# Layer 0 of a four-layer graph kernel: the second diffusion product of a period moved half a period on, block ends moved later in the order, and the guess and the column lists cut into pieces

## The chip, the cores and the metric

The kernel runs on one core of a Trainium2 chip. The time is the device time of the whole program in microseconds; before the change the median of three runs is 3632.99 us (3631.25 to 3634.81).

## The reference

There are N = 4096 nodes with 256 features, and a sparse 4096 x 4096 matrix `adj` (about five entries in a row). Four layers follow each other, each on `h = relu(layernorm(x))` and each added to `x`. The change concerns layer 0 alone, which is cut here to what it computes:

```python
R = S + eye; R = R / R.sum(-1)                 # S is adj
Z = 0; Xf = X; Xa = X
for n in range(2):
    probs = softmax((Xa @ W1.T @ W2.T) @ (Xa @ W3.T).T)
    A = probs * (smallest set of entries of the row that holds 0.9 of its sum)
    A = A / A.sum(-1)
    Xf = R @ Xf                                # diffusion, sparse
    Xa = A @ Xa                                # attention, dense
    Z = Z + Xf @ U1[n].T + Xa @ U2[n].T
out = layernorm(X + Z)
```

The search for the set is what is dear: for each of the 4096 rows of `probs` a threshold has to be found above which 0.9 of the sum lies. Layers 1 to 3 are a graph convolution, a graph attention with four heads and another convolution.

## The kernel before, in words

Layer 0 has two steps, n = 0 and n = 1, each a call of `layer0_step`. A step goes over 32 blocks of 128 rows, and a software pipeline handles five blocks at once. `period(b)` is one turn of it: block b-1 ends, block b is searched exactly and cut, block b+1 gets the upper bound of its threshold, block b+2 is searched by steps, and block b+3 enters. Step 0 has periods -3 to 31, step 1 periods -3 to 33.

The instructions of VectorE (DVE), ScalarE (ACT) and TensorE (PE) stand on each engine in the order in which `period` calls them: these three are under a manual schedule. The orders of GpSimd (POOL) and of SyncE (SP), which issues most DMAs, are made by the scheduler of the language. [...]

What a period does, by engine, with the lines of the kernel before:

- The first search. `exponentials` (L1117, ACT) makes e = exp(logits - guess) of a block, 128 x 4096. `evaluate(b, k)` (L1133, ACT) runs one pass with Sign and one with Relu over e, on 1024 columns for k = 0 and 1 and on all 4096 for k = 2 and 3; each adds up along the row. `update(b, k)` (L1163 to L1203, then `stepped`, L1178 to L1184, DVE) makes the next threshold of both sums; `measured` reads the sum of Sign in L1163 and that of Relu in L1165. `bound` (DVE) makes the upper bound of the threshold.
- The exact search. `below` (L1286, DVE) clears all entries above the bound and writes the 128 x 4096 buffer `near`; `segments` (L1294) takes the eight largest of each of 16 pieces, `listing` (L1305, L1308) sorts the first 48, `decide` finds the last entry kept, `cut` (L1348) and `drop` (L1355) clear the rest of e.
- Attention. `flip(b, g)` (L1395, PE) transposes four 128 x 128 pieces of e, `take` (L1402, ACT) copies them from PSUM, `attend(b, g)` (L1411, PE) multiplies them with the features, for g = 0 to 7. Copies 0 to 3 of a block are made in its own period, copies 4 to 7 in the next one. The copies have three buffers. In step 0 `attended` (L1420, ACT) then scales the product, and `turn`, `next_keys`, `weighted`, `store_xa` and `store_h` make and store what step 1 needs. In step 1 `add_heads` (L1536, DVE) adds the product to a stored sum.
- Diffusion, in step 1 alone. `pair(b)` gives the two blocks that period b diffuses: periods 0 to 15 do the first diffusion (k = 0), periods 17 to 32 the second (k = 1). `reach` gathers the sparse matrix block and the rows that it touches, by indirect DMAs on POOL (L834); it is called two blocks ahead in `mix`, which holds the product (L849, PE). `mixed` (L1513 to L1527, DVE) adds the product to a stored part. For k = 1 `spread` (L1544, ACT) and `finish` (L1553 on DVE, the rest on POOL) normalise the result and store it.

In `period`, both products of a pair are made in the same period: the first after `logits`, the second after `cut`. `spread` and `finish` of the pair before stand ahead of `segments`. Copies 6 and 7 and the products with them stand ahead of the Sign of k = 2:

```python
take(b - 1, (6, 7)); attend(b - 1, 6); attend(b - 1, 7)
for d, k in pair(b - 1):
    if k: spread(d); finish(d)
beside(islice(best, 8), hi)                    # half of the segments
beside(update(b + 2, 1) if new else nothing, hi)
beside(best, hi)
if new: evaluate(b + 2, 2, (AF.Sign,))
if opened: attended(b - 1)                     # step 0
if new: evaluate(b + 2, 2, (AF.Relu,))
```

(Lines are run together here.) `beside(line, *others)` runs one item of each other line after every item of the first; `some(line, k)` runs k items.

Two pieces of work lie around the steps. `guess` makes the first threshold of each block from the second moments of the keys and from all queries: 512 queries at a time are multiplied (L978, PE), combined (L980, DVE) and summed (L985, PE). Its first 512 columns are done at once, and its remaining seven groups in one block after period -3. `listed_columns` lists the non-zero columns of each matrix block from `marks`, which step 0 has collected, in twenty rounds of a maximum and a replacement (L793, L794, DVE). Ten rounds run in `close` at the end of step 0, four after period -3 of step 1, and the rest, with the small operations that make the indices of the gathers, after period -2. `guess` reads all queries from a 128 x 4096 buffer of the pool `e`.

Of the kernel before, what the change touches and what calls it, by code (L numbers as in the profile page):

```python
# [76 lines left out]
P = 128  # L77
N = 4096
# [576 lines left out]
def fast_layers(  # L655
# [304 lines left out]
    def guess(n, pm, qt):  # L960
# [10 lines left out]
        squares, room = {}, e_pool.tile([P, N], F32, name="e")  # L971
        for lo, hi in ((0, 1), (1, 8)):
            for g in range(lo, hi + 1):
                if g < hi:

                    cols = slice(g * 512, (g + 1) * 512)
                    py = ps.tile([P, 512], F32, name="py", tag="pmisc")
                    nc.tensor.matmul(py, mk, qt[:, cols], start=True, stop=True)  # L978
                    squares[g] = room[:, cols]
                    nc.vector.scalar_tensor_tensor(  # L980
                        squares[g], py, mean, qt[:, cols], op0=ALU.add, op1=ALU.mult
                    )
                if g > lo:
                    for r in range(4):
# [6 lines left out]
                        )  # L991
            bs = slice(4 * lo, 4 * hi)
# [20 lines left out]
    def front(h0, kt, xs):  # L1013
# [12 lines left out]
        qt = e_pool.tile([P, N], F32, name="e")  # L1026
        pm = ps1.tile([P, 512], F32, name="pm", tag="pr")
        spread_, scale, shift = (xs.tile([P, NB, k], F32, name=f"x_{k}{i}") for i, k in enumerate((2, 1, 1)))
        turned, pls = {}, {}
# [12 lines left out]
        for i in range(NB + LAG + 4):  # L1042
# [20 lines left out]
            if 0 <= o - 1 < NB:  # L1063
# [5 lines left out]
                nc.vector.tensor_copy(qt[:, b * P : (b + 1) * P], pkq[:, 1, :])  # L1069
                if b % 4 == 3:  # L1070
                    cols = slice((b - 3) * P, (b + 1) * P)
                    nc.sync.dma_start(q_d[0][:, cols], qt[:, cols])
# [8 lines left out]
    def layer0_step(n, va, kt, own, extra=None):  # L1081
# [390 lines left out]
        def next_keys(b, qt=None):  # L1472
# [6 lines left out]
            q = qt[:, cols] if qt is not None else own.tile([P, P], F32, name="q", bufs=2)  # L1479
# [88 lines left out]
        def period(b):  # L1568
# [6 lines left out]
            if n == 1 and b in (0, NB // 2):  # L1575
                reach(0, b // (NB // 2))
                reach(1, b // (NB // 2))
# [6 lines left out]
            if old:  # L1584
# [8 lines left out]
                attend(b - 1, 5)  # L1593
                take(b - 1, (6, 7))
                attend(b - 1, 6)
                attend(b - 1, 7)
            for d, k in pair(b - 1):
                if k:
                    spread(d)
                    finish(d)  # L1600
            beside(islice(best, 8), hi)
            beside(update(b + 2, 1) if new else nothing, hi)
            beside(best, hi)
            if new:
                evaluate(b + 2, 2, (AF.Sign,))
# [17 lines left out]
            )  # L1623
            if next_:
                exponentials(b + 3)
# [14 lines left out]
            for d, k in diffused[1:]:  # L1640
                mix(d, k)
# [22 lines left out]
            extras = [kept(b)] if cur else []  # L1664
            extras += [mixed(d, k) for d, k in diffused[1:]]
# [498 lines left out]
```

## Time and profile before

| | |
|---|---|
| median of three runs | 3632.99 us |
| the profiled execution | 3867.4 us, span 3865.1 us |
| PE, DVE, ACT, POOL busy | 2724.2, 2705.8, 2242.7, 1269.0 us |
| mean granted clock of TensorE | 0.845 |
| first `below` of step 0, first and last of step 1 | 173.8, 1504.3 and 2833.5 us |
| last `below` of step 0 | 1344.7 us |

The times are those of one profiled execution, which is slower than the runs without the profiler. Busy time counts instructions alone; the ends of PE's instructions are modelled. "Idle before" is the time in which an engine had nothing running ahead of an instruction, and the name after the arrow is what released it. A `below` opens each period on DVE, so the periods can be told apart in the trace by line 1286.

### The profile page before, as it was taken

The numbers are of one execution on the slowest core, as the hardware profiler recorded it, in microseconds if no ns is written. First come the engines' busy times: TensorE is split into PE (matmuls) and PEld (weight loads), VectorE is DVE, ScalarE is ACT, GpSimd is POOL, SyncE is SP. The second block draws the span as 40 slices with busy tenths as digits, with TensorE's granted clock in tenths as the row PEclk, the third lists the DMA queues.
The fourth block names the chain that finished last, engine by engine and source line by source line (L and its number), as shares of the span: only waits on it lengthen the run. The fifth ranks groups of instructions, "written<-read, shape, count | busy, mean of one in ns | idle before, by whom it ended". The sixth has DMA issues, their size and how long they took to land. (4 is left out here: it accounts for less than half of the span.)

```text
span 3865.1 us, 43776 instructions
## 1 busy us (share of the span) xinstructions
PE 2724.2 (70%) x12404; PEld 2039.6 (53%) x12404; DVE 2705.8 (70%) x9371; ACT 2242.7 (58%) x3339; POOL 1269.0 (33%) x1342
## 2 busy tenths in 40 slices
PE   6468787877878781677777877767775466688545
PEld 5246565555656550455555655555553354677434
DVE  3399999999999965777778887788754234688200
ACT  3588878888887525666667777677612012577200
POOL 1000000000000003466656435444452663655465
PEclk9688998989899885888889988888887788798777
DMA  3012222121222321233333322222224453444364
GB/s 105 2 56 82 68 76 83 62 86 62 82 70 74 101 76 50 79 90 102 94 89 102 89 60 86 75 86 80 82 69 148 139 167 111 119 125 112 117 186 150
DMA packets 214103, 357.00 MB, mean 92 GB/s; under 512 B 34135, under 2 KB 147292, under 8 KB 213852
## 3 DMA queue, kind: packets, MB, share of 16 engines
q1 hardware_dynamic: 169356, 237.74, 19.3%
q0 software_dynamic: 43520, 116.14, 11.4%
q8 instruction: 101, 1.65, 0.2%
q14 instruction: 150, 1.23, 0.1%
q10 hardware_dynamic: 976, 0.23, 0.0%
HBM read 290.85 MB, written 63.13 MB: 92 GB/s over the span
## 5 line engine op out<-in xcount | busy, mean ns | idle before, releaser
L1133 ACT ACTIVATE unread<-e,next_pair 128x4096 uint8<-128x4096 f32 (+1 forms) x384 | 1097.9, 2859 | 208.6 <-DVE next_pair L1184 103.4
L1402 ACT COPY at<-pat 128x512 f32<-128x512 f32 x512 | 287.3, 584 | 498.9 <-PE pat L1395 205.9
L1411 PE MATMUL pa<-va,at 128*128 128x256 f32 x2048 | 481.4, 391 | 54.4 <-ACT at L1402 49.7
L1411 PE MATMUL pa<-h,at 128*128 128x256 f32 x2048 | 512.5, 411 | 0.0
L1103 PE MATMUL pl<-kt,qb 64*128 64x512 f32 x1024 | 310.6, 716 | 262.8 <-ACT e L1117 174.2
L1411 PEld LDWEIGHTS pa<-h,at 128*128 128x128 f32 x2048 | 423.3, 211 | 63.7
L1411 PEld LDWEIGHTS pa<-va,at 128*128 128x128 f32 x2048 | 392.6, 196 | 112.5 <-ACT at L1402 54.9
L1395 PE MATMUL pat<-ident,e 128*128 128x128 f32 x2048 | 309.2, 298 | 158.7 <-DVE e L1355 90.0
L1296 POOL COPY eighth<-best 128x16 f32<-128x16 f32 x64 | 13.2, 206 | 1215.3 <-DVE best L1294 1181.3
L1294 DVE MAX8 best<-near 128x8 f32<-128x256 f32 x1024 | 407.6, 418 | 4.8
L1395 PEld LDWEIGHTS pat<-ident,e 128*128 128x128 f32 x2048 | 253.9, 153 | 237.2 <-DVE e L1355 120.4
L834 POOL DMA_INDIRECT vg<-v_d,column x320 | 307.2, 960 | 165.2 <-issue 106.0
L849 PE MATMUL acc<-vg,ac 128*128 128x256 f32 x768 | 222.9, 452 | 167.5 <-DVE y L2097 82.3
L849 PE MATMUL pr<-vg,ac 128*128 128x257 f32 (+1 forms) x768 | 244.3, 482 | 133.3 <-DVE h L1522 72.2
L1117 ACT ACTIVATE e<-pl,minus_guess 128x1024 f32<-128x1024 f32 x256 | 282.9, 1111 | 55.6 <-PE pl L1103 28.6
L1103 PEld LDWEIGHTS pl<-kt,qb 64*128 64x128 f32 x1024 | 98.5, 214 | 400.4 <-ACT e L1117 224.4
L849 PEld LDWEIGHTS pr<-vg,ac 128*128 128x128 f32 x768 | 181.3, 243 | 221.6 <-DVE h L1522 91.3
L1286 DVE SCALAR_TENSOR_TENSOR near<-e,end_hi 128x4096 f32<-128x4096 f32 x64 | 286.5, 4477 | 0.1
L1348 DVE SCALAR_TENSOR_TENSOR e<-e,end_t 128x4096 f32<-128x4096 f32 x64 | 286.6, 4478 | 0.0
L849 PEld LDWEIGHTS acc<-vg,ac 128*128 128x128 f32 x768 | 172.8, 232 | 214.5 <-DVE y L2097 85.7
L1355 DVE MATCH_REPLACE8 e<-drop,e 128x4096 f32<-128x4096 f32 x64 | 282.2, 4409 | 0.0
L834 POOL DMA_INDIRECT vg<-mixed_d,column x160 | 210.7, 1317 | 204.8 <-PE pr L853 140.7
(533 smaller groups left out, 4761.7 us busy)
## 6 DMA issues: line engine op xcount, KB each, us to landing
adj<-in_adjt SPq DMA_DIRECT2D x128, 512.0 KB
ac<-adjc_d SPq DMA_DIRECT2D x96, 384.0 KB
adjc_d<-ac SPq DMA_DIRECT2D x32, 384.0 KB
v_d<-v SPq DMA_DIRECT2D x64, 128.0 KB
vg<-v_d SPq DMA_DIRECT2D x64, 128.0 KB
targets<-steep_d SPq DMA_DIRECT2D x32, 256.0 KB
vg<-v_d,column POOLq DMA_INDIRECT x320
table_d<-tab SPq DMA_DIRECT2D x32, 132.0 KB
```

Source lines behind the costliest of these rows:

```text
L834: nc.gpsimd.indirect_dma_start(out, None, rows, bass.IndirectOffsetOnAxis(ap=index, axis=0))
L849: nc.tensor.matmul(acc, ac[:, k, :], v[:, k, :], start=(k == 0), stop=(k == CHUNKS and not own))
L1103: nc.tensor.matmul(pl[:, r, :], s["qb"][rows], kt[rows, j * 512 : (j + 1) * 512], start=True, stop=True,)
L1117: nc.scalar.activation(s["e"][:, j * 1024 : (j + 1) * 1024], pl.rearrange("p r c -> p (r c)"), AF.Exp, bias=minus_guess[:, b : b + 1], acc ...
L1133: nc.scalar.activation(unread[:, :width], s["e"][:, :width], func, bias=s["at"], scale=-1.0, accum_out=s["signs"] if func == AF.Sign else ...
L1286: nc.vector.scalar_tensor_tensor(near, s["e"], end["hi"][:, b : b + 1], s["e"], op0=ALU.is_lt, op1=ALU.mult, accum_out=s["low"])
L1294: nc.vector.max(best[:, k, :], near[:, k * (N // SEG) : (k + 1) * (N // SEG)])
L1348: nc.vector.scalar_tensor_tensor(s["e"], s["e"], last, s["e"], op0=ALU.is_ge, op1=ALU.mult, accum_out=s["held"])
L1355: nc.vector.match_replace(s["e"][:, ::-1], s["drop"], s["e"][:, ::-1], 0.0)
L1395: nc.tensor.transpose(pt[:, k, :], s["e"][:, c * P : (c + 1) * P], ident)
L1402: nc.scalar.copy(at, s["pt", g])
L1411: nc.tensor.matmul(s["pa"], s["at", g][:, k, :], va[:, c, :D], start=(c == 0), stop=(c == NB - 1))
```

## The change

In `period`:

- Copies 6 and 7 of block b-1 and the products with them are called after the Sign of k = 2. `attended` still stands between Sign and Relu in step 0, and now behind them.
- The second product of a pair, `mix`, is called at the end of the period, behind copies 2 and 3; its `mixed` is run in the next period, beside the second half of the segments.
- `spread` and `finish` are called behind `decide`, and ahead of the exponentials.
- The first two `reach` of each diffusion are called after the segments of periods 0 and 16, not at the head of these periods.
- A line `fill` is run in three places of a period, three items in each.

`guess` yields after each group of 512 columns, reads its queries from a buffer of 128 x 512 that it loads from `q_d` (two buffers, the products overwrite them), and keeps the first group in `near`. The lines `guess` and `listed_columns` are run as `fill` in the first periods. `front` and `close` no longer hold a 128 x 4096 buffer of queries. In `front` each group of four blocks is copied to a small buffer that is stored.

```diff
@@ guess
-        squares, room = {}, e_pool.tile([P, N], F32, name="e")
         for lo, hi in ((0, 1), (1, 8)):
+            squares = {}
             for g in range(lo, hi + 1):
                 if g < hi:
-                    cols = slice(g * 512, (g + 1) * 512)
+                    if g == 0:
+                        queries, squares[g] = qt, near[:, 3584:]
+                    else:
+                        queries = squares[g] = wk.tile([P, 512], F32, name="queries")
+                        nc.sync.dma_start(queries, q_d[n][:, g * 512 : (g + 1) * 512])
                     py = ps.tile([P, 512], F32, name="py", tag="pmisc")
-                    nc.tensor.matmul(py, mk, qt[:, cols], start=True, stop=True)
-                    squares[g] = room[:, cols]
+                    nc.tensor.matmul(py, mk, queries, start=True, stop=True)
...
+                    if lo:
+                        yield
@@ period
-        def period(b):
+        def period(b, fill=()):
...
-            if n == 1 and b in (0, NB // 2):
-                reach(0, b // (NB // 2))
-                reach(1, b // (NB // 2))
...
                 attend(b - 1, 4)
                 attend(b - 1, 5)
+            beside(islice(best, 8), hi)
+            beside(update(b + 2, 1) if new else nothing, hi)
+            late = chain(*[mixed(d, k) for d, k in pair(b - 1)[1:]])
+            beside(best, hi, late)
+            some(late, 9)
+            if n == 1 and b in (0, NB // 2):
+                reach(0, b // (NB // 2))
+                reach(1, b // (NB // 2))
+            some(fill, 3)
+            if new:
+                evaluate(b + 2, 2, (AF.Sign,))
+            if old:
                 take(b - 1, (6, 7))
                 attend(b - 1, 6)
                 attend(b - 1, 7)
-            for d, k in pair(b - 1):
-                if k:
-                    spread(d)
-                    finish(d)
-            beside(islice(best, 8), hi)
-            beside(update(b + 2, 1) if new else nothing, hi)
-            beside(best, hi)
-            if new:
-                evaluate(b + 2, 2, (AF.Sign,))
             if opened:
                 attended(b - 1)
...
                 add_heads(b - 1) if old and n == 1 else nothing,
             )
+            for d, k in pair(b - 1):
+                if k:
+                    spread(d)
+                    finish(d)
+            some(fill, 3)
...
                 some(mixed(d, k), 9)
-            for d, k in diffused[1:]:
-                mix(d, k)
...
-            extras = [kept(b)] if cur else []
-            extras += [mixed(d, k) for d, k in diffused[1:]]
-            along(chain(aim(b + 3), update(b + 3, 0)) if next_ else nothing, chain(*extras))
+            for d, k in diffused[1:]:
+                mix(d, k)
+            along(chain(aim(b + 3), update(b + 3, 0)) if next_ else nothing, kept(b) if cur else nothing)
+            some(fill, 3)
@@ the calls
-            period(-3)
-            some(guesses, 2)
-            for b in range(-2, NB):
-                period(b)
+            for b in range(-3, NB):
+                period(b, guesses)
...
+            fill = chain(guesses, lists)
             for b in range(-3, NB + 2):
-                period(b)
-                if b == -3:
-                    some(guesses, 2)
-                    some(lists, 4)
+                period(b, fill)
                 if b == -2:
-                    some(lists, 99)
+                    some(fill, 99)
```

## The prediction

> **What bounds the kernel now.** I read the busy slices first, then busy times by stretch, then the timelines of ScalarE (ACT) and VectorE (DVE) inside one period of each kind. A period opens with the 4.48 us row of line 1286 (`below`). Slices:
>
> ```profile
> PE   6468787877878781677777877767775466688545
> ...
> DVE  3399999999999965777778887788754234688200
> ACT  3588878888887525666667777677612012577200
> ```
>
> Slices are 96.6 us. DVE is full in slices 3 to 13 (step 0 of layer 0), and no engine is in slices 16 to 29 (step 1). Busy time by stretch (PE, PEld, DVE, ACT, POOL, then clock): 23 periods of step 0; step 1's first diffusion; its second diffusion; period 15, which gathers nothing; period 17, where no finished pair is normalised:
>
> ```profile
> 411.10:1274.70 863.60, 694.45 (x3037) 496.85 (x3036) 808.37 (x2877) 701.73 (x875) 10.54 (x69) 0.91 0.23 74
> 1616.40:2241.50 625.10, 478.71 (x2070) 355.79 (x2071) 482.07 (x1812) 427.49 (x481) 363.55 (x306) 0.89 0.33 92
> 2321.20:2750.50 429.30, 317.55 (x1399) 234.94 (x1398) 338.10 (x1251) 296.60 (x361) 201.00 (x221) 0.84 0.28 81
> ...
> 2166.40:2200.90 34.50, 30.43 (x145) 23.60 (x146) 31.56 (x123) 29.34 (x34) 7.27 (x6) 0.95 0.33 102
> 2241.50:2278.10 36.60, 33.22 (x146) 25.95 (x146) 31.61 (x125) 29.31 (x34) 10.58 (x9) 0.85 0.17 47
> ```
>
> So a period takes 863.6/23 = 37.55 us in step 0, 625.1/15 = 41.7 in the first diffusion, 429.3/10 = 42.9 in the second. Step 0, ACT and then DVE (start, duration, group, idle before):
>
> ```profile
> 794.34 0.58 ACT L1402 COPY at<-pat 128x512 f32<-128x512 f32 x1 [1.58 <-PE pat L1395]
> 796.56 0.58 ACT L1402 COPY at<-pat 128x512 f32<-128x512 f32 x1 [1.64 <-PE pa L1411]
> 797.04 3.71 ACT L1133 ACTIVATE unread<-e,next_pair 128x4096 uint8<-128x4096 f32 x1
> ...
> 801.69 0.47 ACT L1420 ACTIVATE xa<-pa,ra 128x256 f32<-128x256 f32 x1 [0.84 <-PE pa L1411]
> 802.06 3.70 ACT L1133 ACTIVATE unread<-e,next_pair 128x4096 uint8<-128x4096 f32 x1
> ...
> 805.88 0.16 DVE L1165 SCALAR_TENSOR_TENSOR next_pair<-twice,gap 128x1 f32<-128x1 f32 x1 [1.70 <-ACT unread L1133]
> ```
>
> The last two copies of a block, Sign, `attended`, Relu stand in that order, and DVE already waits 1.70 us for the Relu. Second diffusion, DVE then ACT:
>
> ```profile
> 2535.84 4.48 DVE L1286 SCALAR_TENSOR_TENSOR near<-e,end_hi 128x4096 f32<-128x4096 f32 x1
> ...
> 2547.88 0.15 DVE L1553 TENSOR_SCALAR var<-var 128x1 f32<-128x1 f32 x1 [7.55 <-ACT junk_sq L1544]
> ...
> 2547.25 0.51 ACT L1544 ACTIVATE junk_sq<-h,minus_mean 128x256 bf16<-128x256 f32 x1
> ...
> 2556.26 3.71 ACT L1133 ACTIVATE unread<-e,next_pair 128x4096 uint8<-128x4096 f32 x1 [7.72 <-DVE next_pair L1184]
> ```
>
> Here `finish` blocks DVE until ACT has copied 6 and 7 and squared; the searches of the next block stand behind it.
>
> [...] here it is 0.50 from 818.5 to 825.3 in step 0, after a window with PE busy 1.09 of 3.4 us, so little work suffices. [...] one during `below` at 1871.8 took 4.22 us against 0.95.
>
> **The change, part by part.**
>
> *A, step 0: copies 6, 7 and the last two products behind the Sign.* Sign needs the DVE update that ended at 796.60 and started at 797.04 behind copy 7: 0.44 us gained, so it ends at 800.4. Copy 6 then ends at 801.0. Products 6 and 7 on PE: 32 matmuls took 7.07, four blocks of columns, so two take 3.54, to 804.6 with the hand-over. `attended`, which stays before the Relu, 0.47 less overlap: 805.0. Relu 3.79: 808.8, plus hand-overs 809.0, against 805.85. That is +3.0 to +3.2 with nothing to hide it: DVE's L1165 stands in order, and `decide`, `cut` (4.48) and `drop` (4.41) queue behind it. The period of 37.55 is 11 clock windows of 3.413 us; 12 would be 40.96, +3.4. I take +3.2. Periods with both the Relu and an old block are 1 to 29: 29 × 3.2 = +93 (lower end 29 × 2.9 = +84; the upper is a rival).
>
> *B, first diffusion, periods 1 to 15.* Removed: the wait of Sign for copy 7 (period 8: update ready at 10.7 us from its start, Sign at 20.4). Added: the second product, 12 matmuls of 2.88 and two of 0.6, less overlap 3.3 us, moves from beside `cut` and `drop` into PE's run from `drop` to product 7. That run, by rows: transposes 8 × 0.52 = 4.1, attention products 8 × 1.77 = 14.2, now 3.3 more, some 21.6 with waits 23. Before, the run to copy 7 (14.7 in period 15) plus 0.5, Sign and Relu (7.5) made 22.7. So the two cancel; PE now also idles some 5 us before `drop` ends, and a cold start costs up to 3.4 (half of the 6.8 us at 0.50). The mixed result (0.65 us of DVE) only moves. The gathers' delays (period 15 without them 34.5, others about 42) are as many as before, elsewhere. I take +0.5 each: +8; bounds -3.5 and +3, so -52 to +45.
>
> *C, second diffusion, periods 18 to 30.* `spread` and `finish` go behind `decide`: the 7.55 + 0.54 us of DVE wait go. ACT has 1.2 us more after the Relu, covered by DVE's 2.2 us of `decide`. Period 17 shows a period without them: 36.6. To it add half of the cold start, 1.7, and 0.7 (an estimate) for GpSimd's eight normalising operations (0.55 to 0.73 each) between DVE's: 39.0. From 42.7 that is -3.7 × 13 = -48, ends -6 (-78) and -2 (-26). Periods 31 to 33: -5. SP's stores of x1 wait for GpSimd later; behind them on SP stand loads of the next period, with some 30 us of room.
>
> *D, between the steps.* Guess pieces took 3.41 us each (paced by PE) and still do; each now also needs a load through SP, two buffers deep, and SP holds the query load of block 0 behind three of them. Ten list rounds of 2.57 now lie under Sign and Relu (7.6) and the exponentials: -15 at the start of period -1. But `reach` now stands behind the segment search of period 0, so 40 gathers at 1.25 us start about 13 us later and delay DVE's dependent operations (1.24 us each from 1538 to 1550) in `listing` and `decide`: +10. I take -5 (-20 to +8). *E, the front and step 0's guess:* the pieces take the time they took; one 512-wide copy more: 0 (-5 to +3).
>
> Sum: +93 + 8 - 48 - 5 - 5 + 0 = **+43**. The profiled execution has a span of 3865.1 us and took 3867.4, 234 above the median of 3633.0; nothing in the page says where the 234 lie, and step 0 and part C show no gather delays, so I carry the difference over unscaled: **3676 us**.
>
> **Rivals.** *R1, faster.* PE's run isn't the limit in the first diffusion: Sign and Relu no longer wait for copy 7 and go on while the gathers delay PE. Place: L1133 behind L1402. For: Sign stood 10 us idle in period 8. Against: product 7 must still end before `add_heads` (L1536), which already waits for PE in nine periods. It decides from 43/15 = 2.9 us below my B, a gain of 2.4 per period; at -3.5 and part C at -6: 93 - 52 - 78 - 10 = -47, 3586. *R2, colder PE in step 0.* Products 4 and 5 end 3 us before copy 6; if that lets the clock fall, products 6 and 7 take up to 3.4 more: 13 windows, 44.4 a period, +6.8 × 29 = +198, in all +148, 3781. For: the fall at 818.5. Against: 3 us is less than a window, busy on both sides. *R3, no change:* B at -2.4 cancels the rest: 3633.
>
> **How the numbers follow.** Mine 0.55 (3635 to 3720), R1 0.22, R2 0.15, R3 0.08. The bound of same, 0.2%, is 7 us, about what a measurement of this kernel can tell. Mine and R2 give slower 0.70; R3 and edges same 0.07; R1 faster 0.23. The range 3590 to 3760 leaves out less than half of R1 and about half of R2, under 2 in 10.
>
> **What would show it.** A right: step 0's period 40.5 to 41, L1165 waiting about 4.8 us, `xa` (L1429 then) waiting over 3 us for PE. B right: about 42 still, PE's wait and not copy 7 ahead of `add_heads`. C right: no wait at `var`, 38 to 40. D right: list rounds between L1165's waits, gathers starting after the first segments. Wrong if `attended` doesn't wait in step 0, if first-diffusion periods fall below 39, or if PE's clock halves twice in a step 0 period.

## The result and the profile after

The changed kernel takes 3825.74 us (median of 4, 3824.95 to 3827.86) against 3632.97 us before: a ratio of 1.0531, 95% interval 1.0513 to 1.0550. It is 193 us slower. The prediction had the sign and not the size: 3676 us, with a range up to 3760.

One thing has to be known before two profiles are laid side by side. The same kernel before took 3632 to 3634 us on three occasions and 3833 to 3863 us on four others. The difference lies in the stages with gathers, step 1 and layers 1 to 3, and not in step 0: where it is there, the text below speaks of a chip with the delay. (No chip stands twice on record, so that it is the chip and not the occasion is likely, and not shown.) The profile of before that the prediction was made from shows the delay; the times of before and all of the changed kernel's above don't. So periods are compared below within one kind of chip alone, and ratios within one group of runs.

The busy slices of the changed kernel (tenths of a slice of 95.6 us, each row one engine; the last row is TensorE's granted clock in tenths):

```profile
PE   6457777777777777736888888888875656688766
...
DVE  3387778888777888858888888888984434588500
ACT  3476667766677765248777777778751311577400
...
PEclk8678888888888888857888888889887889889888
```

DVE had nines through step 0 before. Now no engine has: step 0 waits. The busy time by stretch (length, PE, PEld, which is PE's loading of weights, DVE, ACT, POOL with counts, clock, DMA share, GB/s): 23 periods of step 0, 15 of the first diffusion (periods 2 to 16), 10 of the second:

```profile
451.40:1472.00 1020.60, 772.12 (x3038) 532.00 (x3037) 810.18 (x2877) 703.88 (x875) 10.53 (x69) 0.85 0.20 63
1797.60:2359.30 561.70, 465.10 (x2087) 368.03 (x2088) 474.38 (x1814) 426.95 (x484) 358.60 (x309) 0.86 0.36 104
2430.10:2801.40 371.30, 308.47 (x1401) 244.78 (x1400) 328.31 (x1252) 294.80 (x361) 241.19 (x221) 0.87 0.32 94
```

A step 0 period takes 44.37 us for 37.55, with DVE's work unchanged (810 us for 808 before), and the clock is 0.85 for 0.91. The diffusion periods are 37.4 and 37.1 us. The timeline of ACT, PE and DVE in one step 0 period (start, duration, engine, line, group, idle before and what ended it; the lines are nine higher than before):

```profile
905.26 3.71 ACT L1142 ACTIVATE unread<-e,next_pair 128x4096 uint8<-128x4096 f32 x1 [4.96 <-DVE next_pair L1193]
908.97 1.05 ACT L1411 COPY at<-pat 128x512 f32<-128x512 f32 x2
909.59 6.41 PE L1420 MATMUL pa<-h,at 128*128 128x256 f32 x16 [3.85 <-ACT at L1411]
916.03 0.47 ACT L1429 ACTIVATE xa<-pa,ra 128x256 f32<-128x256 f32 x1 [6.01 <-PE pa L1420]
916.40 3.70 ACT L1142 ACTIVATE unread<-e,next_pair 128x4096 uint8<-128x4096 f32 x1
920.22 0.16 DVE L1174 SCALAR_TENSOR_TENSOR next_pair<-twice,gap 128x1 f32<-128x1 f32 x1 [7.48 <-ACT unread L1142]
```

Before, products 4 to 7 followed each other on PE without a pause, so that two took half of this:

```profile
794.58 7.07 PE L1411 MATMUL pa<-h,at 128*128 128x256 f32 x32
```

Now products 6 and 7 take 6.41 us where the prediction had 3.54, `xa` waits 6.01 us for them between Sign and Relu, and DVE waits 7.48 us for that Relu (1.70 before). In the traces of before and of the changed kernel every stretch of one clock but the last (263 of 264, 347 of 348) lasts a multiple of 3.413 us, so the clock can be read window by window. Four windows of the same period (PE's busy time follows the length; the clock is the last column but two):

```profile
891.20:894.61 3.41, 3.41 (x13) 2.94 (x12) 3.20 (x15) 3.41 (x2) 0.00 (x0) 0.50 0.75 249
904.85:908.26 3.41, 0.88 (x5) 0.43 (x3) 3.41 (x20) 3.00 (x1) 0.00 (x0) 1.00 0.01 2
908.26:911.67 3.41, 2.08 (x5) 1.73 (x6) 3.21 (x19) 1.76 (x4) 0.20 (x1) 0.50 0.00 0
911.67:915.09 3.42, 3.42 (x9) 2.70 (x9) 1.04 (x7) 0.00 (x0) 0.25 (x2) 0.50 0.00 0
```

While copies 6 and 7 stand behind the Sign, PE stands still for 3.85 us, and the clock is at half for the two windows in which it works again. In all, some four of the period's 13 windows are at half clock, where before it was some two of 11 (`b_finish_2` below; the first of the four windows shown is one that has its like there). In the second diffusion DVE's wait for `var` (7.55 us before) is gone, and another stands in its period, for the products that now come late:

```profile
2601.25 0.48 DVE L1545 SCALAR_TENSOR_TENSOR t<-pa,ra,base 128x256 f32<-128x256 f32 x1 [3.98 <-PE pa L1420]
...
2604.50 0.21 DVE L1562 TENSOR_SCALAR var<-var 128x1 f32<-128x1 f32 x2
```

Where the 193 us lie, by the starts of `below` in the profiles (all from chips without the delay; `b_finish_2`, an experiment below, is the kernel before up to its second diffusion, and gives the numbers of before):

| stretch | before | after | difference |
|---|---|---|---|
| to the first `below` | 173.4 | 180.0 | +6.6 |
| step 0, 31 periods | 1169.8 | 1367.1 | +197.3 |
| between the steps, period 0 of step 1 | 206.5 | 215.0 | +8.5 |
| first diffusion, 15 periods | 506.2 | 560.1 | +53.9 |
| second diffusion and the rest | 1571.7 | 1500.9 | -71 |

The last number of before is `b_finish_2`'s 1448.1 us plus the 123.6 us that it is faster than before. The differences sum to 195.

### The profile page after: what moved, and what is told of

It is laid out like the page before. It is cut to its first block, busy times and chain, and to the rows that moved or that the text cites. A ratio compares the mean times of both kernels' runs of the same rounds, so it can differ in the third digit from the quotient of the medians.

```text
span 3823.1 us, 43861 instructions
## 1 busy us (share of the span) xinstructions
PE 2788.5 (73%) x12404; PEld 2085.5 (55%) x12404; DVE 2689.8 (70%) x9372; ACT 2241.6 (59%) x3339; POOL 1308.4 (34%) x1342
## 3 DMA queue, kind: packets, MB, share of 16 engines
q0 software_dynamic: 43520, 116.14, 11.5%
## 5 line engine op out<-in xcount | busy, mean ns | idle before, releaser
L1420 PE MATMUL pa<-h,at 128*128 128x256 f32 x2048 | 575.4, 445 | 113.0 <-ACT at L1411 113.0
L1404 PE MATMUL pat<-ident,e 128*128 128x128 f32 x2048 | 350.9, 328 | 333.1 <-DVE e L1364 269.6
L1420 PEld LDWEIGHTS pa<-h,at 128*128 128x128 f32 x2048 | 460.3, 231 | 202.6 <-ACT at L1411 124.6
L1404 PEld LDWEIGHTS pat<-ident,e 128*128 128x128 f32 x2048 | 291.4, 168 | 420.9 <-DVE e L1364 294.8
L1420 PE MATMUL pa<-va,at 128*128 128x256 f32 x2048 | 500.2, 404 | 0.0
L1420 PEld LDWEIGHTS pa<-va,at 128*128 128x128 f32 x2048 | 414.5, 207 | 60.7 <-ACT at L1411 0.3
L1112 PE MATMUL pl<-kt,qb 64*128 64x512 f32 x1024 | 321.8, 757 | 126.6 <-ACT e L1126 126.6
L834 POOL DMA_INDIRECT vg<-v_d,column x320 | 307.2, 960 | 119.7 <-issue 99.1
L849 PE MATMUL acc<-vg,ac 128*128 128x256 f32 x768 | 233.8, 453 | 88.4 <-DMA vg<-v_d,column 77.6
L834 POOL DMA_INDIRECT vg<-far_d,column x160 | 210.8, 1318 | 181.2 <-DVE near L820 134.5
L2003 PE MATMUL acc<-u,tabg 128*65 128x128 f32 x1536 | 208.3, 291 | 64.2 <-DVE u L1988 62.2
L834 POOL DMA_INDIRECT vg<-mixed_d,column x160 | 204.6, 1279 | 113.6 <-issue 39.3
```

The costliest lines, as they stand in the source:

```text
L834: nc.gpsimd.indirect_dma_start(out, None, rows, bass.IndirectOffsetOnAxis(ap=index, axis=0))
L849: nc.tensor.matmul(acc, ac[:, k, :], v[:, k, :], start=(k == 0), stop=(k == CHUNKS and not own))
L1112: nc.tensor.matmul(pl[:, r, :], s["qb"][rows], kt[rows, j * 512 : (j + 1) * 512], start=True, stop=True,)
L1404: nc.tensor.transpose(pt[:, k, :], s["e"][:, c * P : (c + 1) * P], ident)
L1420: nc.tensor.matmul(s["pa"], s["at", g][:, k, :], va[:, c, :D], start=(c == 0), stop=(c == NB - 1))
```

## Step 0: does the late copy cost it, and is it the clock?

My theory: copies 6 and 7 behind the Sign cost all of step 0's 6.8 us a period, half of it by the clock. The rival: the loss is the clock's alone, or that of `attended` ahead of the Relu.

**b_again** is the kernel before, unchanged.

> The kernel before once more, for a second profile of it: the first one took 234 us longer than its runs. Theory P (in step 0 the late copies and the half clock cost 6.8 us a period, and the first profile of before was delayed in the gathers of step 1 and of layers 1 to 3): a span near 3633, step 0 at 37.55 us a period as in the first profile, the first diffusion near 34.5 instead of 41.7, the second still 42 to 43. Rival Q (the two profiles differ throughout, so that the stages of before and after can't be compared): step 0 other than 37.5.

It took 3830.25 us under the profiler, and the 23 runs of before in its group had a median of 3833.34. So it wasn't the profiler that made the first profile of before longer than the runs. The theory missed, in this.

**a_early** (lines run together):

```diff
+                if n == 0:
+                    take(b - 1, (6, 7)); attend(b - 1, 6); attend(b - 1, 7)
             beside(islice(best, 8), hi)
...
-            if old:
+            if old and n == 1:
                 take(b - 1, (6, 7))
```

> The kernel after, but in step 0 alone copies 6 and 7 and products 6 and 7 stand ahead of the segments again, as before. Theory P: the period of step 0 falls from 44.4 to 37.55, 29 times 6.83 = 198 us less, 3628. Rival Q (other parts of the change, the query buffers or the guess, slow step 0 as well): less than half of that, above 3725.

The period of step 0 is 37.54 us (before 37.55), and the whole 3827.93 us, 0.9984 of before (0.9973 to 0.9994) on a chip with the delay. So this one move is the whole loss of step 0.

**a_warm** puts six products that nothing reads between products 5 and 6.

```diff
+            if opened:
+                warm = ps1.tile([P, 2, D], F32, name="warm", tag="pr")
+                for k in range(6):
+                    nc.tensor.matmul(warm[:, k % 2, :], ident, va[:, k, :], start=True, stop=True)
```

> The kernel after, with six more products of 128x256 on TensorE in step 0 between product 5 and product 6 of each block, into a PSUM buffer that nothing reads: they only keep TensorE busy while copy 6 waits for the Sign. Theory P (3.4 of the 6.8 us are the half clock that the idle time brings): products 6 and 7 take 3.6 instead of 6.4 us, the period is 41.0 and the time 3826 - 29 x 3.4 = 3727. Rival S (the clock is not the cause, the copies' place alone costs 6.8): 44.4 a period and 3826 or more.

The period is 41.4 us (40.6 to 43.1) for 44.4; the ratio is 1.0288 (1.0256 to 1.0320). The timeline of PE and ACT:

```profile
947.97 2.75 PE L1615 MATMUL warm<-h,ident 128*128 128x256 f32 x12
952.25 3.72 PE L1420 MATMUL pa<-h,at 128*128 128x256 f32 x16 [1.52 <-ACT at L1411]
...
956.01 0.47 ACT L1429 ACTIVATE xa<-pa,ra 128x256 f32<-128x256 f32 x1 [3.32 <-PE pa L1420]
```

With the idle stretch down to 1.52 us the clock stays up there (1.00 from 936.4 to 960.3), the two products take 3.72 us, `xa` waits 3.32 us, and the period is 0.4 us over the 40.5 to 41 us that the prediction gave for full clock. So 3 of the 6.8 us are the clock's, and the rival that it is the clock alone falls.

**a_xa_late** leaves the copies late and puts `attended` behind the Relu in step 0.

> The kernel after, but in step 0 the scaling of the attention product stands behind the Relu, so that Relu no longer waits for products 6 and 7; the copies stay late. Theory P (it is this wait in ACT's queue): Relu ends about 19 us into the period, VectorE waits under 2 us for it, the period is 37.5 to 38.5 and the time 3630 to 3660. Rival R (the late products themselves bound the period, through the transposes and stores behind them): 41 or more a period, over 3720.

The period is 41.0 us, not 37.5 (ratio 1.0215, 1.0181 to 1.0249): this gains 3.4 us of the 6.8, in part by the clock, since the two products take 5.41 us there. DVE's wait for the Relu falls to 0.99 us, and the next in the row takes its place (timeline of ACT and DVE):

```profile
955.00 0.37 ACT L1476 COPY hu<-pu 128x256 f32<-128x256 f32 x1 [0.64 <-PE pu L1456]
...
955.40 0.42 DVE L1477 TENSOR_TENSOR hu<-h,pu 128x256 f32<-128x256 f32 x1 [3.43 <-ACT hu L1476]
```

`turn`, the transposes and `weighted` all follow `xa`, and `hu` stands on DVE between `cut` and `drop`. The end of the block is late for whatever comes next, so that the place of `attended` alone isn't the cause either.

## The diffusions: what the moved product costs and the late finish gains

The second group, on a chip with the delay (before: 3850.85 us):

**a_again**, the changed kernel.

> The kernel after once more, beside the others on one chip. Theory P (step 0 loses 6.8 us in each of 29 periods, whatever the chip; the gathers of step 1 and of the later layers are delayed on some chips and not on others): step 0 at 44.4 us a period, 190 to 200 us over before, a ratio near 1.05. Rival H (the loss was one of the chips compared): a ratio within 1 per cent.

It takes 4040.24 us, ratio 1.0481 (1.0451 to 1.0512): 189 us slower there too, so the rival, a loss that only the chips compared had made, falls. Its periods are 44.4, 43.6 and 37.5 us: the first diffusion is slowed by that chip as before's is, the second is not.

**b_finish**, the kernel before with part C alone:

```diff
-            for d, k in pair(b - 1):
-                if k:
-                    spread(d)
-                    finish(d)
             beside(islice(best, 8), hi)
...
                 add_heads(b - 1) if old and n == 1 else nothing,
             )
+            for d, k in pair(b - 1):
+                if k:
+                    spread(d)
+                    finish(d)
```

> The kernel before with one edit: spread and finish behind decide. Theory P (the wait of VectorE for the squares is what the second diffusion loses): its periods fall from 42.5 to 37 or 38, 13 x 5 = 65 us less than before, nothing else moves. Rival I (the gain of after there comes from the moved product or the late copies): still 41 to 43, within 10 us of before.

It takes 3755.70 us, ratio 0.9745 (0.9720 to 0.9771): 95 us faster, twice what part C was given. The second diffusion goes from 43 to 36.1 us a period.

**b_mix_k0**, the kernel before with the second product of the first diffusion alone at the period's end.

> The kernel before with one edit: in the first diffusion the second product of a pair is made at the end of its period, and its mixing runs beside the next segments (the first two gathers of the second diffusion stand behind the segments of period 16, since they read its last rows). Theory P (the product stands in TensorE's run from drop to the last attention product): the first diffusion's periods get 2 to 3.5 us longer, 30 to 50 us over before. Rival J (it is the late copies that lengthen them in after without its late copies in step 0): within 10 us of before.

It takes 3916.15 us, ratio 1.0148 (1.0114 to 1.0181): 65 us slower; 45.8 us a period in the first diffusion where before has 41 (`b_finish`, the same there, has 40.8).

**a_mixback**, the changed kernel with both taken back: copies of step 0 early, products where they were.

> The kernel after with copies 6 and 7 of step 0 early again, and with the second product of both diffusions back beside the first and its mixing back at the end of the period; finish stays late, the copies of step 1 stay late, the guess and the lists stay in pieces. Theory P: the first diffusion's periods are as in before, the second's at 37 to 38, step 0 at 37.5, some 55 us less than before. Rival K (the second diffusion needs the moved product for its gain): its periods 40 or more, and no more than 20 us less than before.

It takes 3774.80 us, ratio 0.9797 (0.9771 to 0.9823): what is left of the change is faster than before, but 19 us slower than `b_finish`. 15 of these are there when the first block of step 1 is cut: the first `below` is at 182.6 us for 175.7, and the stretch between the steps 168.3 us for 158.6 (step 0 is 1.5 us shorter). Its first diffusion, with copies 6 and 7 late and the product where it was, takes 41.8 us a period: on this chip the late copies alone gain nothing there (`b_finish` 40.8), while with the moved product they give back some 2 us (43.6 in `a_again` for 45.8 in `b_mix_k0`).

The third group met a chip without the delay (before: 3632.30 us). **b_finish_2** is `b_finish` again.

> The kernel before with only spread and finish behind decide, once more, to stand beside the others on the same chip and to see it on another chip. Where the gathers delay the operations that wait for them it is 0.972 to 0.977 of before, with 41 us a period in the first diffusion and 35.5 in the second. Where they don't (before near 3633) theory P expects 34 to 35 us a period in the first diffusion, and a smaller gain, 30 to 60 us, since part of before's 42.7 us a period in the second diffusion was the gathers' and not the wait of finish; the rival expects the same 95 us there.

It takes 3508.69 us, ratio 0.9666 (0.9650 to 0.9683). Its two diffusions:

```profile
1583.30:2056.00 472.70, 415.67 (x1962) 320.31 (x1961) 441.33 (x1696) 397.49 (x449) 343.11 (x291) 0.95 0.42 118
2157.70:2495.70 338.00, 299.41 (x1400) 227.26 (x1399) 327.46 (x1251) 294.69 (x361) 245.34 (x220) 0.95 0.36 103
```

These are 14 periods of 33.76 us and 10 of 33.80, now alike. The changed kernel's 37.4 us in the first, which would have passed for a gain against the 41.7 us that the prediction worked with, is a loss of 3.7 us. The gain of part C is larger here, 123.6 us, not smaller as expected; spread over 13 periods it is 9.5 us in each, which would make before's period there 43.3 us. There is no trace of before on such a chip to show that number itself.

**b_again_2**, before once more, was to give it:

> The kernel before once more, for its periods on the chip of the other runs of this group. If its time there is near 3633: 33 to 35 us a period in the first diffusion, and 42 to 43 in the second, where theory P has the whole 124 us that the late finish gained (3632.3 to 3508.7) in 13 periods, 9.5 us in each. The rival: some 38 us a period, and the rest of the gain elsewhere.

It met a chip with the delay again (3861.55 us): 40.96 us a period in the first diffusion, 43.00 in the second. So the 43 us are seen with the delay alone.

Why does the moved product cost 3.7 us a period? Theory: PE, which then has nothing beside `cut` and `drop`, wakes at half clock. Rival: its 3 us now lie in the run of PE from `drop` to product 7. **b_mix** is `b_finish` with the second product of both diffusions moved; its copies 6 and 7 stay early.

> The kernel before with the late finish (b_finish) and with part B whole: the second product of both diffusions at the end of its period, its result mixed in beside the next period's segments. Theory P: PE then stands still for over 5 us beside cut and drop, wakes at half clock, and every period of both diffusions goes from 33.7 to about 37.4 us, as in the changed kernel; 28 periods by 3.7 us, 100 us more than b_finish. Rival H: in the changed kernel the 37.4 us came from the copies of step 1 behind the Sign; then this is within 15 us of b_finish.

It takes 1.0029 of before (1.0013 to 1.0045), where `b_finish` had 0.9745: by the two ratios some 110 us given back, 45.9 and 39.4 us a period for 40.8 and 36.1. The moved product undoes all that part C gains there.

**b_mix_warm** adds 18 products that nothing reads in each diffusion period of `b_mix`.

> b_mix with 18 products of 128x256 that nothing reads (some 4.3 us at full clock) on PE in every diffusion period where the moved product stood, beside cut and drop. Theory P: the clock no longer falls, and the period comes back to 34 to 35 us, most of the 100 us. Rival R: it is the moved product's own 3 us in PE's run between drop and product 7 that makes the period longer; then it stays at 36.5 to 37.5.

It told nothing of the question: 1.0217 (1.0175 to 1.0259), slower still, because the idle products came late and were too long. PE, second diffusion:

```profile
2697.63 10.66 PE L1572 MATMUL warm<-va,ident 128*128 128x256 f32 x34 [2.75 <-DVE h L1522]
```

They waited 2.75 us for their PSUM buffer, which the first product of the pair holds until DVE has read it, so the clock had fallen already (0.50 from 2697.0 to 2703.8); and 18 products are 36 passes (1008 in 28 periods), not 18. **b_mix_fill** mends both: 12 products in a PSUM buffer of the transposes; **b_mix_2** is `b_mix` beside it.

> b_mix again, beside b_mix_fill on the same chip, for its periods there. 39 us in the second diffusion if the gathers delay the others (46 in the first), 37.4 in both if they don't.

> b_mix with idle products on PE where it stands still beside cut and drop, as b_mix_warm meant to have: there they waited 2.7 to 4.1 us for their PSUM buffer behind the mixed result of the first product, and took 9 to 10.7 us where 4.3 were reckoned (18 products are 36 passes of 0.24 us), so that they held up the transposes behind them and the run told nothing. Here 12 products (24 passes, 5.8 us at full clock) in a PSUM buffer of the transposes, which is free by then. Theory P (the clock): the transposes and products 0 and 1 after drop run at full clock, and the period of the second diffusion falls by 1.7 us or more against b_mix on the same chip, in the first diffusion too: 45 to 90 us less in all. Rival R (the moved product's own 3 us in PE's run from drop to product 7): within 0.7 us of b_mix's periods, and within 20 us of its time.

`b_mix_2` takes 1.0047 of before (1.0035 to 1.0059), `b_mix_fill` 1.0027 (1.0014 to 1.0041); they are 5 us apart. The windows in which PE works after `drop`, first `b_mix_2`, then `b_mix_fill`:

```profile
2634.70:2638.11 3.41, 1.44 (x7) 1.44 (x8) 3.41 (x6) 2.41 (x3) 3.23 (x6) 0.50 0.07 18
2638.11:2641.53 3.42, 3.42 (x15) 2.85 (x14) 3.17 (x13) 3.15 (x3) 2.81 (x3) 0.52 0.68 198
```

```profile
2634.91:2638.32 3.41, 2.47 (x16) 1.73 (x14) 3.37 (x9) 3.41 (x4) 3.23 (x6) 1.00 0.10 35
2638.32:2641.74 3.42, 3.42 (x20) 3.07 (x21) 3.21 (x12) 3.42 (x2) 2.81 (x3) 1.00 0.74 221
```

The clock is back, and the period is not (39.2 for 39.4 us). By itself this spoke for the rival. But the timelines of POOL and of ACT show something else that holds this period:

```profile
2613.91 0.95 POOL L834 DMA_INDIRECT vg<-mixed_d,column  x1 [0.30 <-issue]
```

```profile
2615.00 0.59 ACT L1402 COPY at<-pat 128x512 f32<-128x512 f32 x1 [5.20 <-PE pa L1411]
2616.64 0.59 ACT L1402 COPY at<-pat 128x512 f32<-128x512 f32 x1 [1.05 <-remote]
```

Copy 6 starts as the last gather of the period ends (2614.86), 3.2 us after its transposes (2611.78). The profile names products of PE as what released it, but those that its buffer waits for had ended at 2610.91. That chip's gathers set the period, it seems, whatever PE does. So the same idle products went into the changed kernel, whose second diffusion takes 37.1 us without and 37.5 us with the delay: **a_fill**.

```diff
                 some(mixed(d, k), 9)
+            if diffused and next_:
+                heat(11)          # products of 128x256, nothing reads them
             if next_:
                 evaluate(b + 3, 0)
```

> The changed kernel with 11 products of 128x256 that nothing reads (22 passes, some 5.3 us at full clock) on PE in every diffusion period, where PE stands still for 5.4 to 5.9 us beside cut and drop, in a PSUM buffer of the transposes. In b_mix_fill the clock came back and the period did not, but there copy 6 was let go only when the gathers had ended, so that the gathers of that chip set the period; in the changed kernel that copy stands behind the Sign, and its period of the second diffusion was the same 37.4 us on a chip with the gathers' delays (a_again) and on one without. Theory P (the clock): with it up, the second diffusion falls from 37.4 to 35.5 us or less, 20 us or more in all. Rival R (the moved product's own time): 36.8 or more.

It takes 3783.74 us on a chip without the delay, ratio 1.0414 (1.0384 to 1.0445), 42 us less than the changed kernel. First the changed kernel's 14 periods of the first diffusion, then those of `a_fill` and its 10 of the second:

```profile
1797.60:2322.20 524.60, 436.71 (x1960) 345.71 (x1960) 443.21 (x1696) 397.66 (x449) 340.91 (x292) 0.86 0.37 106
```

```profile
1798.23:2298.41 500.18, 469.36 (x2268) 373.83 (x2268) 442.53 (x1696) 396.12 (x449) 339.58 (x292) 0.98 0.39 111
2365.84:2723.77 357.93, 335.05 (x1622) 267.11 (x1623) 328.28 (x1251) 295.21 (x365) 234.06 (x217) 0.98 0.32 94
```

37.47 becomes 35.73 us with the clock at 0.98, and `b_finish_2` has 33.76. So of the 3.7 us the clock has 1.7, and 2.0 stay with the clock up. The second diffusion's 35.8 us lies between the two figures that the expectation set for it (35.5 or less, 36.8 or more): both causes are there, in about equal parts. The late copies of step 1 have no share of the 2.0 us in the first diffusion (`a_whole` below has them, and takes 33.6 us) and 0.6 in the second (34.4). That the rest is the moved product's own time in PE's run is argued, not shown alone. The waits fit it: DVE waits for the last attention product in each of these periods of `a_fill` (44.2 us in the 14, 22.2 us in the 10), and in none of `b_finish_2`'s. But early in that run PE also waits 1.60 us for ACT's copies (at 2616.6 us in `a_fill`), where `b_finish_2` has 0.24 (at 2324.1), so that the product may not have all of it.

## Between the steps, and what is left

**a_whole** is `a_mixback` with the queries kept whole in one tile, as before, so that no piece of the guess loads anything (and `front` stores from that tile again). Pieces, late copies of step 1, late `reach` and late finish stay.

> The changed kernel with the copies of step 0 early and the second product of a diffusion where it was before (as in a_mixback), and besides with the queries kept whole in one tile for the guess of both steps, so that no piece of the guess loads its 512 columns through SP; pieces inside the searches, late copies of step 1, reach behind the segments and the late finish stay. Theory P: part D and part E of the prediction failed on the loads alone, for which PE waits 2.7 to 2.8 us in each piece and 11.6 us once; then the first below comes about 6 us earlier than in a_mixback (near 176 instead of 182.6), the stretch between the steps is 158 to 160 us instead of 168.3, and the whole is 13 to 17 us less than a_mixback's, a ratio to before of about 0.976. Rival: the pieces between the searches themselves cost it; then the stretch stays at 166 to 169 us.

It takes 3478.06 us, ratio 0.9574 (0.9558 to 0.9590), on the chip without the delay: 31 us faster than `b_finish_2`, where `a_mixback` was 19 us slower than `b_finish`. The first `below` comes at 164.1 us, and the stretch between the steps takes 137.2 us (159.5 before, 168.2 changed). PE in the changed kernel, then in `a_whole`:

```profile
1623.12 2.07 PE L982 MATMUL py<-queries,mk 128*128 128x512 f32 x2 [3.31 <-DMA queries<-q_d]
1624.99 1.71 PE L988 MATMUL pst<-halves,queries 128*128 128x2 f32 x8
1638.31 2.08 PE L982 MATMUL py<-queries,mk 128*128 128x512 f32 x2 [11.61 <-DMA queries<-q_d]
```

```profile
1414.38 1.12 PE L978 MATMUL py<-e,mk 128*128 128x512 f32 x2
1415.34 0.95 PE L985 MATMUL pst<-halves,e 128*128 128x2 f32 x8
1416.15 1.10 PE L978 MATMUL py<-e,mk 128*128 128x512 f32 x2
```

In the changed kernel four of the seven later groups of queries wait 2.75 us or more for their load, one of them 11.61 us: its load stands on SP behind eight loads of `va1`, which took 8.47 us to issue. The products behind such a wait run at half clock (2.07 us for 1.12). Without the loads a piece takes 1.75 us at full clock. The pieces were worth some 30 us; the loads, two deep, turned them into a loss of 15.

**b_warm** is `b_finish` with nine idle products in each step 0 period, four behind `turn` and five behind `weighted`.

> The kernel before with only spread and finish behind decide (as in b_finish), and in every period of step 0 that has a block to finish nine products more on PE that nothing reads (each 128x256, about 0.45 us at full clock): four behind turn, where PE stands still for 2.2 us, and five behind the second half of weighted, where it stands still for 2.4 us. Theory P: the two windows at half clock in each period of step 0 of b_finish (861.6 to 865.0 and 885.5 to 888.9) are due to these idle stretches; with them filled the clock stays up, VectorE's waits of 0.67 us for the Relu and 0.95 us for hu go, and as VectorE is busy for 35.3 us of a period the period falls from 37.55 to 36 to 36.5 us, so 30 to 45 us less than b_finish in all. Rival: the period is held by VectorE's own work and the clock's windows, and stays at 37.55; the same time as b_finish. A second rival: the added products delay the wanted ones behind them in PE's order, and the period grows by up to 1 us (30 us more).

It takes 3468.40 us, ratio 0.9547 (0.9531 to 0.9563), 40 us less than `b_finish_2`. The stretch of 451.40 to 1201.90 in it has

```profile
451.40:1201.90 750.50, 657.66 (x3103) 467.69 (x3102) 728.65 (x2597) 631.28 (x789) 9.58 (x63) 1.00 0.24 77
```

a clock of 1.00 and periods of 36.2 us, of which DVE is busy for 35.15. So the 37.55 us of before weren't DVE's work alone: about 1.4 us of them hung on the two windows at half clock.

**b_best** puts `b_warm` and the pieces of `a_whole` together, with the copies of step 1 early.

> What the runs so far leave: the kernel before with the late finish, the guess in pieces inside the searches but from queries kept whole in one tile, the list in pieces, reach behind the segments, and the nine idle products of b_warm in each period of step 0; copies and second products as before. Expected, if these gains add up (before near 3633): b_finish 3509, less 31 (the pieces, as in a_whole), less 40 (step 0, as in b_warm), less up to 8 (late copies of a_whole taken back in step 1): 3430 to 3445. The rival: they share a cover, and it stays above 3455.

It takes 3687.26 us against 3863.36 on a chip with the delay, ratio 0.9534 (0.9497 to 0.9570), 176 us less. Step 0 has 36.2 us a period, the stretch between the steps 132 us, the first `below` is at 159.6 us. This chip has the delay, so the total that was expected can't be compared; the parts up to step 1 add up (the last `below` of step 0 is 54 us earlier than in `b_again_2`), while the first diffusion lost some of it (41.7 for 41.0 us a period).

## Why the prediction was right and wrong

*A, step 0.* The chain was right at every joint: Sign, copies, two products, `attended`, Relu, DVE. Its failed step is the term "so two take 3.54". They took 6.41, at half clock. Rival R2 had named just this, with 13 windows of the clock and 44.4 us a period; 44.37 was measured, and its +198 us against +197. It was given 0.15 on the argument that 3 us is less than a window, though no trace had shown that the clock needs a whole window of standstill to fall, and its own sum, 3781, lies outside the range that was stated (as R1's 3586 does). The number against that argument stood in the prediction itself: the fall of the granted clock at 818.5 (0.50 up to 825.3), after a window with PE busy for 1.09 us. Here the window ahead had 0.88. In neither of the two did PE stand still throughout. The rival should have been the forecast. Of the 152 us by which the differences in the table exceed the prediction's +43, this term has 104, B 46, D and E 20, and C with periods 31 to 33 takes 18 off.

*B.* "So the two cancel" failed on both kinds of chip. Taking away the wait of Sign for copy 7 gains next to nothing by itself (41.8 us a period for 40.8 with the delay, 33.6 for 33.8 without). With the delay the two together cost 2.8 us a period (43.6 for 40.8), close to the upper bound of 3; on the chip of the times they cost 3.7 us, 54 us in all, beyond the upper bound of 45, and the base is 33.8 us where B was sized against 41.7. And the second diffusion had a share of it: 33.8 to 37.1 us, where part C's sum held 1.7 us of clock and no more.

*C.* The mechanism was right: DVE's wait for `var` is gone. The mis-sized term is the floor: "Period 17 shows a period without them: 36.6" plus 1.7 and 0.7. That period's own clock was 0.85, so its 36.6 us held half clock already before 1.7 was added for it. Alone the late finish reaches 36.1 us with the delay and 33.8 without (there at a clock of 0.95), and gains 95 to 124 us, not 48. B then took some 43 back (3.3 us in 13 periods), and 5 more in period 16, so the changed kernel shows -71 from there to its end. That this lies inside C's bounds (-78 to -26) is luck: a gain and a loss were both put too small.

*D and E.* "Guess pieces took 3.41 us each (paced by PE) and still do" failed twice: the 3.41 us were half clock, and the added load, named in the same sentence, was put at nothing. +8.5 and +6.6 us for -5 and 0, the one just outside its bound (+8), the other well outside (+3); each is read from single profiles. That `reach` would cost 10 us didn't show: period 0 of step 1 is 46.8 us, 47.0 without it.

*The carry-over.* "nothing in the page says where the 234 lie, and step 0 and part C show no gather delays" was half right: step 0 has none. But against the table's numbers of before that profile is 116 us longer in the first diffusion, 27 in period 0 of step 1, and some 92 from period 16 of step 1 to the end; and R1 and B were argued from the first diffusion. (The prediction's 4.22 us against 0.95 is one gather on GpSimd, L834 at 1872.90 us. In that profile 46 of 960 gathers took over 1.5 us, 2.71 to 5.21, each beside a `below`, `cut` or `drop`; in that of the changed kernel 46 of 960 as well.)

*The signs named.* The clock in step 0 was named as a sign, "if PE's clock halves twice in a step 0 period". It halves three times in the changed kernel, but in `b_again`, whose step 0 is before's and takes 37.54 us, it halves twice already, so that the sign could not tell; the count of windows at half clock can. First-diffusion periods below 39 us, named as the sign of R1, came too, and mean the opposite on this chip.

What step 0 turned into is a pause in each turn of a loop, behind which the next products start at half clock. 3.85 us did it in the changed kernel, and with 1.52 us (`a_warm`) it didn't happen. By the count in the last section (under 1.4 us of work in a window of 3.413) some 2 us are enough if they lie in one window, by my estimate.

## What to carry to other kernels

Before moving products on PE, write down how long PE will stand still ahead of them, and price them at half clock if that leaves a window of 3.413 us with under some 1.4 us of work (counted for this kernel and its variants in the next section); a few products that nothing reads, in a stretch that is idle anyway and a PSUM buffer that is free, are the test and may be the cure. Cutting a block of work into pieces is worth what it hides only if its inputs don't become a chain of loads through a busy queue (here waits of 2.75 to 11.61 us). And where an unprofiled median and a profile differ by several per cent, find the stage that holds the difference before any stage is priced from that profile.

## What the runs showed of the hardware that was not expected

- The clock fell also after windows in which PE had worked (0.88 and 1.09 of 3.413 us above). In the 20 traces here, from 150 to 2800 us of each and with PE's busy time as the profile has it, each of the 1767 windows of 3.413 us at full clock in which PE was busy for under 1.4 us was followed by one at half clock; of the 9141 with 1.7 us or more, 7 were. A window at half clock was never followed by one at full when PE was busy in it for under 2.5 us (1746 windows), and mostly was with 2.9 us or more (1897 of 1997). The traces of before and of the changed kernel alone have 183 of 183 windows, 1 of 837, 0 of 215 and 202 of 212.
- Among the exceptions is a TensorE that stays at half clock without a pause. In the guess of `b_finish` the profile has PE busy throughout, with pairs of 128x512 products and eight of 128x2:

```profile
1429.65:1433.07 3.42, 3.42 (x11) 2.38 (x10) 0.75 (x1) 0.00 (x0) 0.00 (x0) 0.50 1.03 305
1433.07:1436.48 3.41, 3.41 (x11) 2.38 (x10) 0.75 (x1) 0.00 (x0) 0.00 (x0) 0.50 0.83 236
1436.48:1439.89 3.41, 3.41 (x11) 2.38 (x10) 0.75 (x1) 0.00 (x0) 0.00 (x0) 0.50 0.00 0
```

  Six such windows follow each other (1426.24 to 1446.72), and the clock is 0.50 in all of them. In `a_whole` the same pairs, behind the products of `weighted` (L1449, 3.76 us) and then among logits, take 1.75 us a group for 3.41, with the clock at 1.00 from 1410.24 to 1427.30. Why is open.
- Where the clock falls in each turn, the period often settled on whole windows of 3.413 us: 37.55 (11), 40.96 (12, `a_xa_late`) and 44.37 (13) in step 0, and 37.5 in the changed kernel's first diffusion without the delay and its second with it. It left them as soon as the clock stayed up (36.2 and 35.8 us). It is no rule: the second diffusion of `b_mix` takes 39.4 us, 11.5 windows, with one fall in each.
- The kernel before takes 3632 to 3634 us on some chips and 3833 to 3863 on others, with step 0 the same to 0.01 us a period and the first diffusion at 33.8 us or at 40 to 42. The gathers themselves take the same on both (a median of 0.95 us on GpSimd in `b_finish` and in `b_finish_2`), so the difference isn't in how long one takes. What makes it on one occasion and not on another is open.
